# First keys loaded a step before first values, and two signs moved from the first network into the attention

## Chip, core and metric

One core of a Trainium2 chip runs the whole kernel. The metric is the device time in microseconds; of the kernel before, three runs are known, with a median of 729.78 us (726.8 to 729.82).

## What is computed

The reference is a gated block in two layers on x, 8 batches of 256 rows of 512:

```
x = x + tanh(g_xattn[0]) * L0_xattn(ctx, ctx, layernorm(x))   # long convolution of k*v, times q
x = x + tanh(g_ffn[0])   * L0_ffn(layernorm(x))                # 512 -> 1408 -> 512, ternary weights
x = x + tanh(g_xattn[1]) * L1_xattn(layernorm(x), ctx, mask)   # softmax over 256 context rows
x = x + tanh(g_ffn[1])   * L1_ffn(layernorm(x))                # 512 -> 2048 -> 512, one-bit weights
```

The last network uses `sign(w) * mean(|w|)` for each of its weights w1, w2 and w3. So signs of 3 x 2048 x 512 weights must be made at some time before it, and for w3 the sum of absolute values too. The attention of a batch needs the context twice: transposed as keys (cT) and as values (cN).

## The kernel before

The kernel keeps x in SBUF as 16 tiles of 128 rows (NT = 16) and goes through four stages: the convolution over 32 heads, the first network, the attention, the second network. The order of instructions is written out by hand: the program calls them in the order in which each engine is to run them, and every engine works through its own list in order. Engines wait for each other through semaphores only.

**The first network** is the loop over t from 0 to 16 (from L996). In step t TensorE makes the up products of tile t (`up_block`, L860, three blocks of columns 0, 512 and 1024), ScalarE applies SiLU (L868), VectorE multiplies (L869). In the same step the hidden rows of tile t - 1 are quantised: VectorE finds their maximum and the scale (L518 to L522), ScalarE rounds (L1019), POOL clips (L1037), SP starts a DMA transpose (`hqT`, L1039). One step later they are multiplied down (`down0`, L877), and one step after that added to x (`residual`, L228). In step 16 the attention's first work is mixed in: the table for Exp is loaded (L211), and the scores of tiles 0 and 1 (L951) are made between the last up product and the down product of tile 14. The down product of tile 15 follows in step 1 of the attention.

**The signs.** `w1_signs(k)` (L838) issues on SP the load of piece k, 256 KB, into one of three buffers (`p_st`, L844), and returns a function that lets ScalarE make the signs (L848) and, for the 16 pieces of w3, the sum of absolute values (L850). There are 48 pieces. Each step from 3 to 15 loads two, and the step after makes their signs; the last two, loaded in step 15, are made in the attention. The attention takes its number of loads per step from the list `SIGNS` and makes in step t what was loaded in step t - 1. In steps 1 to 15 one sign comes after eT, before the exponentials, and the others come at the end of the step.

**The attention** is a loop over t from 0 to 17 (from L1202). A full step has on TensorE: the transposes of the exponentials of tile t - 1 (L972), the scores of tile t (L951), the transposes of the normalised x of tile t + 2 (L940) and the readout of tile t - 1 (L980). ScalarE has eT (L974), a sign, the exponentials (L966), the normalised x of tile t + 3 (L201), and another sign. In the steps in `BY_POOL` the normalised x is made by POOL instead (L932). Keys and values of a batch serve two tiles and have two buffers each; those of batch t/2 + 1 are loaded in even and odd steps (L899, L904), the masks two batches ahead by POOL's own DMA (L909).

All loads, the transposes and the stores share SP's one queue and its order; masks go through POOL's queue. The lines that the change touches are L1044 (keys and values of batch 0, in step 14), L1083 (pool opened in step 13), L1088 (loads of pieces) and L1199 to L1200 (`SIGNS`, `BY_POOL`).

Of the kernel before, what the change touches and what calls it, by code (L numbers as in the profile page):

```python
# [23 lines left out]
NT = B * S // P  # L24
# [18 lines left out]
def flamingo_gated_kernel(  # L43
# [17 lines left out]
    def pool(stack, name, bufs, **kw):  # L61
        return stack.enter_context(tc.tile_pool(name=name, bufs=bufs, **kw))
# [146 lines left out]
    def load_table(func):  # L209

        nc.scalar.activation(junk1, ln_eps, func)  # L211
# [303 lines left out]
    def row_max(v, tag):  # L515

        am = small.tile([P, 1], F32, tag="am" + tag, name="am")
        nc.vector.tensor_reduce(am, v, AX.X, ALU.max, apply_absolute_value=True)  # L518
        inv = small.tile([P, 1], F32, tag="inv" + tag, name="inv")
        nc.vector.tensor_scalar(inv, am, Q_EPS, 1.0 / 127.0, ALU.max, ALU.mult)  # L520
        sc = small.tile([P, 1], F32, tag="sc" + tag, name="sc")
        nc.vector.reciprocal(sc, inv)  # L522
        return inv, sc

    def front_norm(k):
        xn0[k] = pf.tile([P, L], F32, tag="xn", name="xn2")
        if k < GRP:
            ln_apply_act(xn0[k], order0[k], *firsts[k // 2], k % 2)
        else:
            ln_apply_act(xn0[k], order0[k], *st0[k // GRP][1:], k % GRP)  # L530

    def front_max(k):
        am0[k] = row_max(xn0[k], "x")
# [320 lines left out]
    def up_block(xqT, f1, hh, f0):  # L854
        fw = min(512, FF0 - f0)
        pa = ps_mm.tile([P, 512], F32, tag="mm", name="pa")
        pb = ps_mm.tile([P, 512], F32, tag="mm", name="pb")
        for i, pp in ((0, pa), (1, pb)):
            for c in range(NL):
                nc.tensor.matmul(  # L860
                    pp[:, :fw],
                    xqT[:, c, :],
                    w0q[i][:, c, f0 : f0 + fw],
                    start=(c == 0),
                    stop=(c == NL - 1),
                )
        sl = p2.tile([P, 512], F32, tag="sl", name="sl")
        nc.scalar.activation(sl[:, :fw], pa[:, :fw], AF.Silu, scale=f1[:, 0:1])  # L868
        nc.vector.scalar_tensor_tensor(  # L869
            hh[:, f0 : f0 + fw], pb[:, :fw], f1[:, 1:2], sl[:, :fw],  # L870
            op0=ALU.mult, op1=ALU.mult,
        )
# [24 lines left out]
    def load_keys(b):  # L897
        cT = p3.tile([P, NL, S], F32, tag="cT", name="cT")
        nc.sync.dma_start(out=cT.rearrange("p c m -> p (c m)"), in_=ctx_t[b])  # L899
        return cT  # L900

    def load_values(b):
        cN = p3.tile([P, S // P, L], F32, tag="cN", name="cN")
        nc.sync.dma_start(out=cN, in_=ctx_n[b].rearrange("(c p) d -> p c d", p=P))  # L904
        return cN
# [13 lines left out]
    def batch_gate(neg):  # L919

        valid = small.tile([P, 1], F32, tag="valid", name="valid")
        nc.vector.tensor_reduce(valid, neg, AX.X, ALU.max)
        gv = small.tile([P, 1], F32, tag="gv", name="gv")
        nc.vector.tensor_scalar(gv, valid, 0.0, gate_x[1], ALU.is_equal, ALU.mult)
        return gv

    def normalised3(t, by_pool=False):
        xn = p3.tile([P, L], F32, tag="xn", name="xn3")
        rstd, nmr = st3[t // GRP][1:]
        if by_pool:  # L930
            c = slice(t % GRP, t % GRP + 1)
            nc.gpsimd.tensor_scalar(xn, xs[:, t, :], rstd[:, c], nmr[:, c], ALU.mult, ALU.add)  # L932
        else:
            ln_apply_act(xn, t, rstd, nmr, t % GRP)
        return xn
# [12 lines left out]
    def scores(xT, cT):  # L948
        ps = ps_mm.tile([P, 512], F32, tag="mm", name="ps")
        for c in range(NL):  # L950
            nc.tensor.matmul(  # L951
                ps[:, :S], xT[:, c, :], cT[:, c, :], start=(c == 0), stop=(c == NL - 1)
            )
        return ps
# [41 lines left out]
    for t in range(NT + 1):  # L996
        new = t + 2 < NT
        if t < NT:
            hh = p2.tile([P, FF0], F32, tag="hh", name="hh")
        if new and t > 0:  # L1000
            front_norm(t + 2)
        if t > 1:
            inv, sc = row_max(h_[t - 1], "h")
        if t == NT:
            xn_[2] = normalised3(2)
            load_table(AF.Exp)
            gates3 = {0: batch_gate(negs[0])}
            ps_ = {k: scores(xT_.pop(k), keys[0]) for k in range(2)}
        if t < NT:
            up_block(*x0[t], hh, 0)  # L1010
        if t == 0:
            front_norm(t + 2)
        if t == 1:

            ln_finish(*FINISH[0])
            inv, sc = row_max(h_[0], "h")
        if 1 <= t:
            q = p1.tile([P, FF0], I8, tag="i8h", name="i8h")
            nc.scalar.activation(q, h_.pop(t - 1), AF.Copy, scale=sc)  # L1019
        if t == NT - 2:  # L1020
            xn_ = {k: normalised3(k) for k in range(2)}
        if t >= 3:
            residual(order0[t - 3], *d_.pop(t - 3))
        back = BACK.get(t, [])
        if len(back) == 3:
            sums.append(odd_back(odds[back[0]]))
        if new:
            front_max(t + 2)
        if t < NT:
            up_block(*x0[t], hh, 512)  # L1030
        if t == NT - 1:
            xT_ = {k: x_transposed(xn_.pop(k), True) for k in range(2)}
        if new:
            front_int(t + 2)
        if 1 <= t:
            b = p2.tile([P, FF0], BF16, tag="qh", name="qh0")
            nc.gpsimd.tensor_scalar(b, q, 127.0, -128.0, ALU.min, ALU.max)  # L1037
            bT = p_hq.tile([P, NF0, P], BF16, tag="hqT", name="hqT")
            nc.sync.dma_start_transpose(out=bT, in_=b)  # L1039
            f3 = small.tile([P, 1], F32, tag="f3", name="f3")  # L1040
            nc.gpsimd.tensor_scalar(f3, inv, gw0, None, ALU.mult)
            hq_[t - 1] = (bT, f3)
        if t == NT - 2:
            keys, values = {0: load_keys(0)}, {0: load_values(0)}  # L1044
        if new:
            front_turn(t + 2)
        for add in sums:
            add()
        sums = []
        if back:  # L1050
            sums.append(odd_back(odds[back[-2]]))
        if t > 2:
            hqT, f3 = hq_.pop(t - 2)
            d_[t - 2] = (down0(hqT), f3)
        if t in FINISH and t > 0:
            ln_finish(*FINISH[t])

        for k in STATS3.get(t, ()):
            ln_moments_of(st3, natural, k, "3")
        if t > 0:  # L1060
            for k in STATS0.get(t, ()):
                ln_moments_of(st0, order0, k, "0")
        if t < NT:
            up_block(*x0.pop(t), hh, 1024)
            h_[t] = hh
        if t == 2:

            hqT, f3 = hq_.pop(0)
            d_[0] = (down0(hqT), f3)
        if back:  # L1070
            sums.append(odd_back(odds[back[-1]]))
        for add in sums:
            add()
        sums = []
        if t == 0:
            clip_by_act(2, 3)
        if t == 3:
            s_conv.close()
            wp1 = pool(ctx, "w1", 1, reuse_waits="tile")
            w1q = [wp1.tile([P, NL, FF1], F32R, name=f"w1_{i + 1}") for i in range(2)]  # L1080
            p_st = pool(s_att, "w1st", 3, reuse_waits="tile")
        if t == NT - 3:
            p3 = pool(s_att, "p3", 2, reuse_waits="tile")  # L1083
        if t < NT:
            for make in signs:
                make()
            signs = []
        if 3 <= t < NT:  # L1088
            signs = [w1_signs(made + k) for k in range(2)]
            made += 2  # L1090
        if t == NT - 2:
            bytes_ = {b: load_mask(b) for b in range(2)}
        if t == NT - 1:
            negs = {0: key_mask(bytes_.pop(0))}
        if t == NT:
            negs[1] = key_mask(bytes_.pop(1))
# [99 lines left out]

    SIGNS = [0, 2, 2, 2, 2, 1, 2, 1, 1, 2, 1, 1, 2, 2, 1]  # L1199
    BY_POOL = {5, 7, 10}  # L1200
    e_, r_ = {}, {}
    for t in range(NT + 2):  # L1202

# [32 lines left out]
        if t + 3 < NT:  # L1236
            xn_[t + 3] = normalised3(t + 3, t in BY_POOL)
        if t > 0:
# [37 lines left out]
        if t == NT:  # L1276
            mean_w1(2)
            nc.vector.tensor_scalar(gw1, wmean1[:, 2:3], gate_f[1], None, ALU.mult)
        if t < len(SIGNS):
            signs += [w1_signs(made + k) for k in range(SIGNS[t])]  # L1280
            made += SIGNS[t]
        if t == NT - 4:
# [217 lines left out]
```

## Time and profile before

| | |
|---|---|
| Median of three runs | 729.78 us |
| The profiled execution, as timed | 731.69 us |
| Its span in the trace | 729.8 us, granted TensorE clock 0.992 |
| ScalarE busy | 371.6 us (51%) |
| Up products of the first network, first to last | 181.1 to 299.5 us |
| Last down product of the first network (in the attention) | 312.3 to 314.9 us |
| Scores of the attention, first to last | 300.5 to 369.1 us |
| Signs (L848) | 48 of 0.62 us, from 220.5 to 371.7 us |
| DMA moved | 99.36 MB, mean 136 GB/s |

Times are measured from the start of the span. In a timeline, a row gives the start, the time, the engine, the source line, the operation, what it writes and reads, and in brackets how long the engine sat idle ahead of it and whose event ended that. In the rows of SP the time is that of issuing; when the bytes arrive is in the trace's DMA records. The chain of waits is followed back from the end of the program: each row is the work, or the wait for a transfer, that the next row could not start without.

### The profile page before, as it was taken

The numbers are of one execution on the slowest core, as the hardware profiler recorded it, in microseconds if no ns is written. First come the engines' busy times: TensorE is split into PE (matmuls) and PEld (weight loads), VectorE is DVE, ScalarE is ACT, GpSimd is POOL, SyncE is SP. The second block draws the span as 40 slices with busy tenths as digits, with TensorE's granted clock in tenths as the row PEclk, the third lists the DMA queues.
The fourth block names the chain that finished last, engine by engine and source line by source line (L and its number), as shares of the span: only waits on it lengthen the run. The fifth ranks groups of instructions, "written<-read, shape, count | busy, mean of one in ns | idle before, by whom it ended". The sixth has DMA issues, their size and how long they took to land.

```text
span 729.8 us, 10128 instructions
## 1 busy us (share of the span) xinstructions
PE 713.4 (98%) x3200; PEld 532.0 (73%) x3200; DVE 598.6 (82%) x1224; ACT 371.6 (51%) x669; POOL 260.8 (36%) x366
## 2 busy tenths in 40 slices
PE   7999999999899999899999999999999999999997
PEld 6777777777454444556668888888888888888885
DVE  5799888999788888777868988988888988777965
ACT  5577887879777777657652222322222332212322
POOL 4788997989874535245300020000200002000000
PEclk8999999999999999999999999999999999999999
DMA  5775676831136565797704455544553444554443
GB/s 196 238 240 159 188 266 202 281 85 32 35 84 139 141 142 141 159 279 219 225 27 96 103 110 110 115 96 110 113 115 83 110 103 104 118 110 91 102 90 86
DMA packets 149970, 99.36 MB, mean 136 GB/s; under 512 B 83806, under 2 KB 127838, under 8 KB 149918
## 3 DMA queue, kind: packets, MB, share of 16 engines
q1 hardware_dynamic: 149608, 98.38, 51.2%
q0 software_dynamic: 256, 0.26, 1.0%
q8 instruction: 25, 0.41, 0.2%
q14 instruction: 27, 0.22, 0.1%
q10 hardware_dynamic: 54, 0.08, 0.1%
HBM read 75.58 MB, written 5.03 MB: 110 GB/s over the span
## 4 chain that ended last, share of the span: by engine, by line
PE 82%; DVE 5%; DMA 4%; POOL 3%; issue 3%; ACT 2%; SPq 0%; DVEq 0%; ACTq 0%; POOLq 0%
PE y L349 17%; PE po L1375 16%; PE pb L1181 15%; PE pa L1181 15%; PE po L877 4%; PE pa L860 4%; PE pb L860 4%; PE po L980 2%; PE ps L951 2%; DMA w1st<-in_L_w3t 2%; DMA hqT<-qh 1%; POOL kv L326 1%; PE tr L416 1%; POOL prod L394 1%; DMA sT<-d 1%
## 5 line engine op out<-in xcount | busy, mean ns | idle before, releaser
L349 PE MATMUL y<-kv,toep 128*128 128x288 f32 x640 | 161.1, 409 | 0.9 <-DVE prod L384 0.7
L349 PEld LDWEIGHTS y<-kv,toep 128*128 128x128 f32 x640 | 120.1, 191 | 33.5 <-ACT qx L313 0.9
L1189 ACT ACTIVATE sl<-pa,wmean 128x512 f32<-128x512 f32 x64 | 44.0, 688 | 195.1 <-PE pa L1181 195.1
L1375 PE MATMUL po<-w,lo 128*128 128x512 f32 x256 | 99.9, 390 | 0.0
L1375 PE MATMUL po<-w,hi 128*128 128x512 f32 x256 | 99.6, 389 | 0.0
L181 POOL TENSOR_TENSOR nwt<-rstd 128x4 f32<-128x4 f32 x33 | 6.6, 199 | 235.1 <-DVE rstd L176 233.2
L326 POOL TENSOR_TENSOR kv<-cx 128x1024 f32<-128x1024 f32 x32 | 60.6, 1895 | 24.2 <-ACT cx L313 24.0
L1181 PE MATMUL pa<-w,hi 128*128 128x512 f32 x256 | 69.2, 392 | 0.0
L1181 PE MATMUL pb<-w,hi 128*128 128x512 f32 x256 | 68.6, 390 | 0.1
L1181 PE MATMUL pa<-w,lo 128*128 128x512 f32 x256 | 68.5, 389 | 0.0
L1181 PE MATMUL pb<-w,lo 128*128 128x512 f32 x256 | 68.4, 389 | 0.0
L860 PEld LDWEIGHTS <-xqT 128*128 128x128 bf16 x384 | 37.9, 99 | 41.2 <-issue 3.1
L394 POOL TENSOR_TENSOR prod<-prod 128x1024 f32<-128x1024 f32 x28 | 66.3, 2368 | 0.0
L1155 ACT CAST hi<-v 128x512 fp32r<-128x512 f32 x64 | 39.2, 622 | 47.9 <-DVE v L1365 47.9
L1193 DVE SCALAR_TENSOR_TENSOR hh<-pb,wmean,sl 128x512 f32<-128x512 f32 x64 | 47.8, 747 | 14.7 <-PE pb L1181 14.5
L1375 PEld LDWEIGHTS po<-w,lo 128*128 128x128 f32 x256 | 48.0, 188 | 10.9 <-DVE lo L1160 1.0
L1181 PEld LDWEIGHTS pa<-w,hi 128*128 128x128 f32 x256 | 47.8, 188 | 10.8 <-ACT hi L1155 0.6
L1181 PEld LDWEIGHTS pb<-w,hi 128*128 128x128 f32 x256 | 48.0, 188 | 10.5 <-DVE hh L1193 0.6
L1181 PEld LDWEIGHTS pa<-w,lo 128*128 128x128 f32 x256 | 48.1, 188 | 10.0
L1375 PEld LDWEIGHTS po<-w,hi 128*128 128x128 f32 x256 | 48.1, 188 | 9.9
L1181 PEld LDWEIGHTS pb<-w,lo 128*128 128x128 f32 x256 | 48.0, 188 | 10.0
L371 DVE TENSOR_TENSOR prod<-y,qx 128x512 f32<-128x512 f32 x64 | 43.8, 684 | 8.6 <-ACT y L359 4.4
(163 smaller groups left out, 1345.3 us busy)
## 6 DMA issues: line engine op xcount, KB each, us to landing
sT<-d SPq DMA_DIRECT2D x64, 256.0 KB
toep<-ssm_skip SPq DMA_DIRECT2D x31, 256.0 KB
ch<-in_ctx_heads SPq DMA_DIRECT2D x32, 128.0 KB
w1a<-in_L_w1t SPq DMA_DIRECT2D x8, 512.0 KB
w1a<-in_L_w2t SPq DMA_DIRECT2D x8, 512.0 KB
w1st<-in_L_w1t SPq DMA_DIRECT2D x16, 256.0 KB
w1st<-in_L_w2t SPq DMA_DIRECT2D x16, 256.0 KB
cT<-in_ctx_t SPq DMA_DIRECT2D x8, 512.0 KB
```

Of the source, the lines that this page charges most:

```text
L326: nc.gpsimd.tensor_tensor(kv[:, :, 0 : ND * HD].rearrange("p a (i d) -> p a i d", d=ND), cx[:, :, 0:HD].unsqueeze(3).to_broadcast([P, NL * ...
L349: nc.tensor.matmul(y[:, k, :, W0 : W0 + NPAIR], toeps[h][:, d * P : (d + 1) * P], kvs[h][:, mi * B : (mi + 1) * B, :].rearrange("p b n -> ...
L371: nc.vector.tensor_tensor(prod[:, 0, r, :, :], yv[:, :, W0 : W0 + ND * HD].rearrange("p a (i d) -> p a i d", d=ND), view(q, [HX, n], [1, H ...
L394: nc.gpsimd.tensor_tensor(flat[0], flat[0], flat[1], ALU.add)
L860: nc.tensor.matmul(pp[:, :fw], xqT[:, c, :], w0q[i][:, c, f0 : f0 + fw], start=(c == 0), stop=(c == NL - 1),)
L877: nc.tensor.matmul(po, hqT[:, c, :], w0q[2][:, c, :], start=(c == 0), stop=(c == NF0 - 1))
L951: nc.tensor.matmul(ps[:, :S], xT[:, c, :], cT[:, c, :], start=(c == 0), stop=(c == NL - 1))
L1155: nc.scalar.copy(hi, v)
L1181: nc.tensor.matmul(pp, xT[k][:, c, :], w1q[i][:, c, f0 : f0 + 512], start=(c == 0 and k == 0), stop=(c == NL - 1 and k == 1),)
L1189: nc.scalar.activation(sl, pa, AF.Silu, scale=wmean1[:, 0:1])
L1193: nc.vector.scalar_tensor_tensor(hh, pb, wmean1[:, 1:2], sl, op0=ALU.mult, op1=ALU.mult)
L1375: nc.tensor.matmul(po, hT[b][k][:, c, :], w1q[2][:, b * NL + c, :], start=(b == 0 and c == 0 and k == 0), stop=(b == NB - 1 and c == NL - ...
```

## The change

Four edits. The keys of batch 0 are loaded at the end of step 13, before that step's two pieces, instead of in step 14 just before the values. Step 14 loads no pieces, so step 15 makes no signs, and every later piece is loaded and made by a later entry of the lists. `SIGNS` has one load more in step 0 and one more in step 5. POOL makes the normalised x of attention step 6 instead of that of step 5.

```diff
         if t == NT - 2:
-            keys, values = {0: load_keys(0)}, {0: load_values(0)}
+            values = {0: load_values(0)}
...
         if t == NT - 3:
             p3 = pool(s_att, "p3", 2, reuse_waits="tile")
+            keys = {0: load_keys(0)}
         if t < NT:
             for make in signs:
                 make()
             signs = []
-        if 3 <= t < NT:
+        if 3 <= t < NT and t != NT - 2:
             signs = [w1_signs(made + k) for k in range(2)]
             made += 2
...
-    SIGNS = [0, 2, 2, 2, 2, 1, 2, 1, 1, 2, 1, 1, 2, 2, 1]
-    BY_POOL = {5, 7, 10}
+    SIGNS = [1, 2, 2, 2, 2, 2, 2, 1, 1, 2, 1, 1, 2, 2, 1]
+    BY_POOL = {6, 7, 10}
```

The pieces that each step loads, before and after:

| | step 13 | 14 | 15 | attention 0 | 1 to 4 | 5 | from 6 |
|---|---|---|---|---|---|---|---|
| before | 20, 21 | 22, 23 | 24, 25 | none | 26 to 33 | 34 | 35 on |
| after | 20, 21 | none | 22, 23 | 24 | 25 to 32 | 33, 34 | 35 on |

Pieces 16 to 31 are of w2, those from 32 on of w3. The number of instructions on each engine stays the same.

## The prediction

> **What bounds the kernel now.** I read the page first, then the chain of waits in order of time, then the timelines of single engines in the stretch that the diff touches.
>
> ```profile
> span 729.8 us, 10128 instructions
> PE 713.4 (98%) x3200; PEld 532.0 (73%) x3200; DVE 598.6 (82%) x1224; ACT 371.6 (51%) x669; POOL 260.8 (36%) x366
> ```
>
> TensorE fills 98% of the span, so a change without a matmul in it can only win where TensorE waits. The order of TensorE's and of VectorE's instructions is the same in both kernels; only the orders on ScalarE (ACT), SyncE (SP) and GpSimd (POOL) differ. The chain of waits leaves TensorE twice between 299 and 313 us, where the first network's last steps (t = 15 and 16) meet the attention:
>
> ```profile
> 299.02 5.36 DMA hqT<-qh
> ...
> 304.43 2.55 PE po L877 x11
> ...
> 308.75 3.50 DMA hqT<-qh
> ...
> 312.30 2.56 PE po L877 x11
> ```
>
> Two transposes of the quantised hidden rows each hold back a down product (L877). The second row, on an empty queue, takes 3.50 us; the first takes 5.36. The SP timeline says what lay ahead of it, and when each was issued:
>
> ```profile
> 290.52 1.39 SPq L1039 DMA_TRANSPOSE hqT<-qh  x1
> 291.95 0.84 SPq L899 DMA_DIRECT2D cT<-in_ctx_t  x1
> 292.85 0.43 SPq L904 DMA_DIRECT2D cN<-in_ctx_n  x1
> 293.37 1.72 SPq L844 DMA_DIRECT2D w1st<-in_L_w2t  x2
> 299.02 2.10 SPq L1039 DMA_TRANSPOSE hqT<-qh  x1
> 301.21 2.15 SPq L844 DMA_DIRECT2D w1st<-in_L_w2t  x2
> ```
>
> Keys, values and two sign pieces (512+512+256+256 KB, section 6 of the page) are issued within 3.2 us, behind a transpose. The trace's DMA records show their bytes moving from about 295 to 302.5 us; the keys' last part lands at 300.37, the pieces at 302.36 and 303.05, and the transpose only after them at 304.38. The timelines of TensorE, ScalarE and VectorE show who waits:
>
> ```profile
> 300.50 3.69 PE L951 MATMUL ps<-cT,xT 128*128 128x256 f32 x16 [0.65 <-DMA cT<-in_ctx_t]
> 312.30 2.55 PE L877 MATMUL po<-w,hqT 128*128 128x512 bf16 x11 [1.14 <-DMA hqT<-qh]
> ```
> ```profile
> 302.38 1.32 ACT L848 ACTIVATE w<-w1st 128x512 fp32r<-128x512 f32 x2 [2.56 <-DMA w1st<-in_L_w2t]
> 303.61 0.80 ACT L201 ACTIVATE xn<-xs,nmr,rstd 128x512 f32<-128x512 f32 x1
> 304.43 1.28 ACT L211 ACT_TABLE_LOAD   x1
> 305.72 0.20 ACT L211 ACTIVATE junk<-ln_eps 128x1 f32<-128x1 f32 x1
> 305.83 1.45 ACT L1019 ACTIVATE i8h<-hh,sc 128x1408 int8<-128x1408 f32 x1
> ```
> ```profile
> 302.45 0.17 DVE L522 RECIPROCAL sc<-inv 128x1 f32<-128x1 f32 x1
> ```
>
> The cause of the second stall is in the middle fence. ScalarE works in order: two signs wait 2.56 us for their pieces, and behind them queue a normalisation, the table load and the last quantisation (L1019). The scale it needs was ready at 302.62, but it starts at 305.83, 3.2 us late, and through POOL (L1037) it makes the last transpose as late.
>
> **The change part by part.** The sum is made against the profiled execution, span 729.8 us, 731.69 us as timed; the median of the three runs shown is 729.78 (726.8 to 729.82), so a span saving is taken off 729.78.
>
> *The two signs of step 14.* Their loads (293.37) and their ScalarE work (302.38, with the wait) leave this place. After the last activation of step 15 (L868, 299.24 to 299.72) ScalarE goes on with xn 0.7, table 1.28 and junk 0.2, so it is free by 302.0, and the quantisation starts when its scale is there: 302.62 + 0.10 (the step before: scale done 295.98, start 296.08) = 302.72. POOL starts 1.56 later (296.08 to 297.64 before), the transpose is issued 1.38 after that (297.64 to 299.02): 305.66. It lands 3.50 later at 309.16 and its product starts at 309.2 instead of 312.30: **3.1 us** earlier. Here a rule speaks against the sum. The Trainium skill, page "ScalarE: Activation LUTs", section "What ACT_TABLE_LOAD costs", charges a switch of table at 1283 ns plus a drain of 1380 ns. By it ScalarE would be free at 303.3, past the scale, and the saving would be 2.5 us, an estimate. The trace has the load at 304.43, 0.02 after the 0.80 row in front of it, and the next row 1.29 later: no drain shows, so I take 1.28.
>
> *Does TensorE get there in time?* Scores (L951) can start when the last up block ends (299.04 + 0.65) and ScalarE's xT (second copy done by 299.1) is there: 299.72 instead of 300.50, provided the keys are present. Sixteen matmuls at 3.44 back to back (300.50 to 303.94) end at 303.16. The first delayed transpose, issued at 299.02 on a queue that holds only values by then, takes the 3.50 of the empty-queue row and lands at 302.5, so the down product runs 303.16 to 305.54, 1.27 earlier than now. Then transposes of xn (0.44), of the exponentials (0.22; their maximum is ready on VectorE at 304.84, the exponentials at 305.4), the next transposes when VectorE has emptied the bank (306.87), and the readout 307.44 to 309.16. So TensorE is free at 309.2 too. The two bounds meet; 3.1 us stands, and what is late next is either.
>
> *The keys a step ahead.* Issued at about 286.4, ahead of step 13's two pieces. There the cost is bounded by the hole in the queue:
>
> ```profile
> 290.00:292.00 2.00, 2.00 (x13) 1.12 (x12) 0.93 (x2) 1.80 (x4) 1.89 (x4) 1.00 0.15 30
> ```
>
> The last columns are DMA share and GB/s. Before, step 13's pieces landed at 289.87 and 290.49 (landing records). 512 KB more at the 400 GB/s that this trace's full half-microseconds show is 1.3 us, so they land at 291.2 and 291.8. ScalarE takes them at 291.71 and some 0.5 later; behind them on ScalarE stand the first activation of step 15 (292.75) and then 2.64 us of idling before L1019, which covers it. The transpose issued at 290.52 shows its first packets at 291.69 anyway; it landed by 295.01, its product starts at 296.01. Bounds: nothing, and, if the 1 MB needs twice the 4.1 us that 0.5 MB took from issue to landing, a product up to 1.7 us late. I take nothing, since the hole is there in the row. A gain beyond the 0.78 counted is excluded, because scores need xT. SP's other passed entry is the mask load on POOL, which is not moved.
>
> *The signs in the attention.* Sixteen steps of 4.1 us on TensorE (0.22 + 1.73 + 0.44 + 1.72 in the chain). Two pieces more: one loaded in step 0, one in step 5, so step 1 makes three signs and step 6 two. A sign is 0.62, with its absolute sum 1.45 (L848, L850). Step 6 loses a normalisation (0.80) to POOL (0.77), step 5 gets it back and swaps one w3 piece for a w2 piece. Step 5 on ScalarE then is 0.62 + 1.45 + 0.80 + 0.70 + 0.36 = 3.9 and step 6 is 2.9 + 0.70 + 0.36 = 4.0, both under 4.1. In step 1 the third sign waits for its piece, issued behind the next keys: it lands about 311.5, the sign ends near 312.4, and eT behind it is due for the readout at 313.9. Cover 1.1 us, so nothing on the path; if the piece came 2 us later, 0.9. On SP, step 1's loads wait until signs free their buffers (to about 311), and behind them stand the keys of the third batch, first read in step 4, some 10 us on. POOL's mask load of step 6 now stands behind the moved normalisation, 0.8 us later. That bears on these waits:
>
> ```profile
> 342.35 0.63 ACT L848 ACTIVATE w<-w1st 128x512 fp32r<-128x512 f32 x1 [1.62 <-DMA w1st<-in_L_w3t]
> 359.58 0.63 ACT L848 ACTIVATE w<-w1st 128x512 fp32r<-128x512 f32 x1 [2.14 <-DMA w1st<-in_L_w3t]
> ```
>
> TensorE lost 0.28 at the first (344.28 against 344.00) and 0.76 at the second (361.51 against 360.75). The packets of mask and piece overlap between 338 and 341. A later mask lets the first piece pass: a gain of 0.28, else at worst 0.5 more loss. I take the gain, since the piece's own queue is short there. The second is left as it is. Sum: 3.1 + 0.3 = 3.4 us, 729.78 - 3.4 = **726.4 us**.
>
> A second rule bears on the queue. "DMA: Bandwidth & Descriptors", in "Rules for kernel authors", says that a transpose next to ordinary DMAs needs nothing. That concerns order, not time: read as free company, the first transpose would gain nothing from an emptier queue. The rows say 5.36 behind the bulk, 3.50 without. By the rule read so, the down product stays at 304.43, the readout ends 1.2 later, and the total gain is about 2.2; by the rows 3.4. I take the rows.
>
> **Rivals.**
> *More than that:* with masks and loads falling otherwise, both attention waits vanish, and with them the 0.38 us before 319.33: 3.1 + 0.28 + 0.76 + 0.38 = 4.5, so 725.3. For it: these waits are accidents of one engine's late packets. Against: their buffers turn over as before.
> *Given back to bandwidth:* 512 KB move from a network step into the attention, where 310 to 330 us already runs at some 270 GB/s. If that is the limit, 1.9 us come back and 1.5 remain: 728.3. Against: SP there mostly waits for ScalarE to free a buffer, not for bytes.
> *Slower:* all three sign buffers are full when the attention starts, so every load waits for the sign before it, and every sign of steps 1 to 7 for its load; ScalarE, in order, holds up eT and the exponentials. At the 0.76 of the 359.58 row, seven steps cost 5.3, net +1.9: 731.7; at the whole 2.14, +11.6. It decides from 0.49 us a step. For it: such waits exist in the trace. Against: in steps 2 to 5 of before, with the same two pieces a step, just one such wait (317.33) shows, with no TensorE idling behind it.
> *It does not do what it says:* step 13's traffic delays the 290.52 transpose by 1.7 and the rest moves with it: net 1.7, 728.1.
>
> **How the numbers follow.** 0.5% is 3.65 us, about what a measurement of this kernel can tell from no change, so 726.13 and 733.43 are the borders. Main case 726.4 with its own range 725.4 to 727.4, chance 0.47, a little under half beyond the border. More: 0.30, all beyond. Bandwidth or step 13: 0.10. Slower: 0.13, somewhat over half within 0.5%. Faster 0.22 + 0.30 = 0.52; slower 0.06; the rest, 0.42, same. The range takes in 'more' with the 3 us by which the runs shown differ, half of it below: 723.8; above it reaches past bandwidth into the slower case's lower half: 730.0.
>
> **What would show it.** Right: no w1st wait on ScalarE near 302, L1019 started near 302.7, scores near 299.7, the last two down products near 303.2 and 309.2. Step 13 is wrong if the product at 296.01 waits. The attention is wrong if L848 rows in its first eight steps show DMA waits with TensorE idling at tre (L972) behind them.

## The result and the profile after

| | before | after |
|---|---|---|
| Median | 729.82 us (13 runs, 726.8 to 732.12) | 726.0 us (13 runs, 724.78 to 728.54) |
| Profiled execution, as timed | 731.69 us | 727.47 us |
| Its span | 729.8 us | 725.6 us |

The ratio is 0.9959, with a 95% interval of 0.9944 to 0.9973: a saving of 3.0 us (2.0 to 4.1) where 3.4 was forecast; the two medians lie 3.8 us apart, inside that interval. It can be measured, and the best estimate is less than 0.5%.

From the page of the kernel after, the head and the busy time of the engines (the two instructions more than before are no engine's work: the counts behind each x are the same):

```profile
span 725.6 us, 10130 instructions
...
PE 710.6 (98%) x3200; PEld 530.8 (73%) x3200; DVE 598.7 (83%) x1224; ACT 371.5 (51%) x669; POOL 260.1 (36%) x366
```

The chain of waits in order of time (start, length, what):

```profile
301.76 2.37 PE po L877 x11
...
305.91 1.72 PE po L980 x4
307.67 2.56 PE po L877 x11
...
331.84 6.96 DMA w1st<-in_L_w3t
338.83 0.64 ACT w L848
339.49 0.72 ACT w1st L850 x2
340.21 0.50 ACT s L966 x2
340.76 0.44 PE tre L972 x2
```

Both `hqT` transfers are gone from it: through the last two down products of the first network the chain stays on TensorE, but for one copy by ScalarE (0.38 us, L974). But one new transfer has come in, at 331.84: a piece of w3, whose late arrival holds ScalarE and then TensorE at 340.76.

The timeline of ScalarE around the table load, then that of SP (time of issue), then that of TensorE:

```profile
298.17 0.80 ACT L201 ACTIVATE xn<-xs,nmr,rstd 128x512 f32<-128x512 f32 x1
298.99 1.28 ACT L211 ACT_TABLE_LOAD   x1
300.29 0.20 ACT L211 ACTIVATE junk<-ln_eps 128x1 f32<-128x1 f32 x1
301.16 1.47 ACT L1019 ACTIVATE i8h<-hh,sc 128x1408 int8<-128x1408 f32 x1 [0.67 <-DVE sc L522]
```
```profile
297.48 1.37 SPq L1039 DMA_TRANSPOSE hqT<-qh  x1
298.90 1.27 SPq L844 DMA_DIRECT2D w1st<-in_L_w2t  x2
304.10 1.39 SPq L1039 DMA_TRANSPOSE hqT<-qh  x1
```
```profile
298.14 3.62 PE L951 MATMUL ps<-cT,xT 128*128 128x256 f32 x16
301.60 2.54 PE L877 MATMUL po<-w,hqT 128*128 128x512 bf16 x11
...
307.67 2.55 PE L877 MATMUL po<-w,hqT 128*128 128x512 bf16 x11
...
314.70 0.44 PE L972 MATMUL tre<-ident,s 128*128 128x128 f32 x2 [0.38 <-ACT s L966]
...
340.76 0.44 PE L972 MATMUL tre<-ident,s 128*128 128x128 f32 x2 [1.22 <-ACT s L966]
```

The quantisation L1019 no longer stands behind two signs. ScalarE is free early and waits 0.67 us for VectorE's scale. The scores and both down products have no idle time in brackets ahead of them.

**How the profiles are compared.** This profile reaches the down product of tile 12 at 286.47, that of before at 288.01, long ahead of anything the change touches. So I count from that product on. The table shows how much earlier (minus) TensorE started its work than in the first profile of before. "Before again" and "after again" are second profiles of the same two kernels; "tre k" are the transposes of the exponentials of tile k (L972), made in attention step k + 1.

| | before again | after | after again | keys only | signs only | signs late | few masks | masks on SP |
|---|---|---|---|---|---|---|---|---|
| scores (L951) | +0.26 | -0.82 | -0.82 | -0.82 | -0.82 | +0.02 | -0.82 | -0.82 |
| down product, tile 14 | +0.30 | -1.29 | -1.29 | -1.29 | -1.29 | +0.07 | -1.29 | -1.29 |
| down product, tile 15 | +0.32 | -3.09 | -3.08 | -1.68 | -3.10 | -1.92 | -3.10 | -3.08 |
| tre 2 | +0.32 | -3.09 | -3.04 | -1.68 | -3.10 | -1.94 | -3.10 | -2.73 |
| tre 8 | +0.05 | -1.98 | -1.61 | -1.83 | -2.15 | -2.21 | -3.38 | -3.02 |
| second network, first up product | -0.76 | -2.80 | -2.42 | -2.65 | -2.97 | -3.09 | -4.25 | -3.89 |

Two things are to be read in it. By tile 15 the change brings 3.09 us in both profiles, counted from the first profile of before; counted from before again, whose own stretch is 0.3 us longer, it is 3.4. By tre 8 it has lost 1.1 (2.0 left) and 1.5 (1.6 left) of that again.

### The profile page after: what moved, and what is told of

It reads as the page before. It is cut to its first block, busy times and chain, and to the rows that moved or that the text cites. A ratio compares the mean times of both kernels' runs of the same rounds, so it can differ in the third digit from the quotient of the medians.

```text
span 725.6 us, 10130 instructions
## 1 busy us (share of the span) xinstructions
PE 710.6 (98%) x3200; PEld 530.8 (73%) x3200; DVE 598.7 (83%) x1224; ACT 371.5 (51%) x669; POOL 260.1 (36%) x366
## 4 chain that ended last, share of the span: by engine, by line
PE 92%; DVE 2%; DMA 2%; ACT 2%; issue 1%; POOL 0%; SPq 0%; DVEq 0%; ACTq 0%; POOLq 0%
PE y L349 22%; PE po L1376 16%; PE pb L1182 15%; PE pa L1182 15%; PE po L877 5%; PE pa L860 5%; PE pb L860 5%; PE ps L951 3%; PE po L980 3%; DMA w1st<-in_L_w3t 1%; PE tr L416 1%; PE tr_back L424 1%; PE tr L940 1%; DMA sT<-d 1%; DMA ch<-in_ctx_heads 1%
```

## Experiments: the two bounds at the first network's end

The theory: two signs in ScalarE's order cost the last down product 3.1 us, the loads ahead of the first transpose cost the first one 1.3. The rivals put the gain on the keys alone, or see the move of the loads as needless.

**Keys only.** Before, with this edit alone:

```diff
         if t == NT - 2:
-            keys, values = {0: load_keys(0)}, {0: load_values(0)}
+            values = {0: load_values(0)}
...
         if t == NT - 3:
             p3 = pool(s_att, "p3", 2, reuse_waits="tile")
+            keys = {0: load_keys(0)}
```

> The kernel before with one edit: the keys of batch 0 loaded in step 13, signs and lists as before. Theory (the gain is the emptied queue and the freed ScalarE, and the two signs of step 14 cause both): moving 512 KB away brings step 14's two pieces and the first transpose some 1.3 us forward, so ScalarE's wait near 302 shrinks from 2.56 to about 1.3, scores start 0.7 earlier, the first of the two last down products 1.2 earlier, the second 1.3 earlier. Total 1.3 us, ratio 0.998. Rival (the keys are the gain, since the scores wait for them): the whole 3.1 us, ratio 0.996.

Measured: 729.51 us (20 runs) against 730.0, ratio 0.9988 (0.9971 to 1.0005), so the times alone don't show a gain. In the profile the two down products come 1.29 and 1.68 earlier, where 1.2 and 1.3 were expected. The timeline of ScalarE, then that of TensorE:

```profile
298.86 1.32 ACT L848 ACTIVATE w<-w1st 128x512 fp32r<-128x512 f32 x2 [0.89 <-DMA w1st<-in_L_w2t]
...
300.91 1.28 ACT L211 ACT_TABLE_LOAD   x1
...
302.31 1.45 ACT L1019 ACTIVATE i8h<-hh,sc 128x1408 int8<-128x1408 f32 x1
```
```profile
308.78 2.55 PE L877 MATMUL po<-w,hqT 128*128 128x512 bf16 x11 [1.13 <-DMA hqT<-qh]
```

The signs now wait 0.89 us instead of 2.56, because their pieces no longer queue behind the keys. But they still stand ahead of L1019, and the last transpose still stops TensorE for 1.13. So 1.41 of the 3.09 us stay lost as long as the signs stand there.

**Signs only.** Before, with the other edits and the keys left in step 14:

```diff
-        if 3 <= t < NT:
+        if 3 <= t < NT and t != NT - 2:
...
-    SIGNS = [0, 2, 2, 2, 2, 1, 2, 1, 1, 2, 1, 1, 2, 2, 1]
-    BY_POOL = {5, 7, 10}
+    SIGNS = [1, 2, 2, 2, 2, 2, 2, 1, 1, 2, 1, 1, 2, 2, 1]
+    BY_POOL = {6, 7, 10}
```

> The kernel before with the signs of step 14 moved (and the two lists as in the changed kernel), keys still beside the values in step 14. Theory: with 512 KB less in the queue the keys land before 299.7 anyway (they are first in it), the transpose on an empty queue takes 3.5 us, the last quantisation starts when its scale is ready: the second down product 3.1 us earlier, as in the changed kernel, ratio about 0.996. Rival (the keys matter by themselves): scores still wait 0.65 us and the gain is 2.4 or less.

Measured: 729.03 us (20 runs), ratio 0.9976 (0.9961 to 0.9992). All rows of the table down to the second down product are those of after, to 0.01 us. So in the profile moving the signs gives the whole 3.1, and moving the keys then adds nothing: without the two pieces the keys are there by 300.03, and the scores start at 300.30 with no idle time. The times leave this less certain: a ratio of about 0.996 was expected, and 0.9976 is nearer to no change than the 0.9959 of after, though the two intervals overlap.

**Signs late.** Before, with only ScalarE's order changed: the two signs of step 14's pieces, which stood in step 15, go behind L1019. Every load stays where it was.

```diff
             nc.scalar.activation(q, h_.pop(t - 1), AF.Copy, scale=sc)
+            if t == NT:
+                signs.pop(0)()
+                signs.pop(0)()
...
-        if t < NT:
+        if t < NT - 1:
             for make in signs:
                 make()
             signs = []
         if 3 <= t < NT:
-            signs = [w1_signs(made + k) for k in range(2)]
+            signs += [w1_signs(made + k) for k in range(2)]
```

> The kernel before with all loads where they were; only the making of step 14's two pieces on ScalarE moves from before the table load to just behind the last quantisation (L1019). Theory: the quantisation starts at 302.7, so ScalarE's share of the gain appears without the queue's: the first transpose still takes 5.4 us and holds the first product at 304.4, the second product is bounded by TensorE at about 310.4, 1.9 us earlier. Rival (the queue is the whole cause, ScalarE's order only follows): no gain, 0.0 us.

Measured: 728.7 us (20 runs), ratio 0.9972 (0.9955 to 0.9989). The first down product does not move (+0.07), the second comes 1.92 earlier. The timeline of ScalarE:

```profile
303.26 1.47 ACT L1019 ACTIVATE i8h<-hh,sc 128x1408 int8<-128x1408 f32 x1 [0.68 <-DVE sc L522]
```

L1019 starts as soon as the scale is there, as in after, but TensorE comes to the last product only at 310.9, since the first transpose still lands late behind the bulk. This separates the two bounds: a new order on ScalarE with the old loads gives 1.92, the keys out of the way with the old order (which shortens the signs' wait too) 1.68, both bounds together 3.09. It is no sum; the later of the two counts each time.

## Experiments: the loss at attention step 9

TensorE's list between tre 7 and tre 8 is 4.10 us long. What it took beyond that: before 0.28 and 0.02 in its two profiles, keys only 0.13, signs late 0.00, all with the old lists; after 1.39 and 1.72, signs only 1.23, all with the new lists. ScalarE's row ahead of it in after (its timeline), then one from the attention's start, for comparison:

```profile
338.83 0.63 ACT L848 ACTIVATE w<-w1st 128x512 fp32r<-128x512 f32 x1 [2.73 <-DMA w1st<-in_L_w3t]
```
```profile
310.91 0.63 ACT L848 ACTIVATE w<-w1st 128x512 fp32r<-128x512 f32 x1 [1.24 <-DMA w1st<-in_L_w2t]
```

The wait at 310.91 is that of the third sign in step 1. TensorE has nothing in brackets behind it. The wait at 338.83 is too long to hide: behind it in ScalarE's order stand the exponentials (L966) whose transposes TensorE needs. This piece is loaded in step 7, and its signs are made in step 8, so it is called the piece of step 7 below.

**Few masks.** After, with the mask loads of batches 2 to 7 left out; those batches use the masks of batches 0 and 1.

```diff
             if b < B:
                 keys[b] = load_keys(b)
-            if b + 1 < B:
-                bytes_[b + 1] = load_mask(b + 1)
...
-                negs[b + 1] = key_mask(bytes_.pop(b + 1))
+                negs[b + 1] = key_mask(bytes_[(b + 1) % 2])
```

> The changed kernel with the mask loads of batches 2 to 7 left out: every later batch takes the mask of batch 0 or 1 again, so six of eight masks are not the reference's. In the changed kernel ScalarE waits 2.73 us at 338.83 for the first piece of attention step 7 and TensorE idles 1.22 us behind it. Theory (the mask packets of POOL's queue slow that piece): the wait falls under 1 us, TensorE idles under 0.3 us, the total falls by about 1 us against the changed kernel. Rival (the piece is late because its buffers turn over late, or by chance of one DMA engine): wait and idling stay.

Measured: 726.15 us (19 runs), ratio 0.9946 (0.9929 to 0.9963): 3.9 us below before (2.7 to 5.2), where after is 3.0 below (2.0 to 4.1). The loss is 0.00, and no wait for w3 is left in the attention. The windows view shows what happens while a mask comes in. Last two columns: DMA share and GB/s. First this kernel, then after, whose TensorE is at the same place to 0.03 us:

```profile
334.00:335.00 1.00, 1.00 (x4) 0.46 (x3) 1.00 (x2) 1.00 (x3) 0.00 (x0) 1.00 1.05 404
335.00:336.00 1.00, 1.00 (x6) 0.72 (x5) 0.86 (x6) 0.97 (x5) 0.00 (x0) 1.00 0.96 309
```
```profile
334.00:335.00 1.00, 1.00 (x4) 0.50 (x3) 1.00 (x2) 1.00 (x3) 0.00 (x0) 1.00 1.20 152
335.00:336.00 1.00, 1.00 (x7) 0.68 (x5) 0.86 (x6) 0.97 (x4) 0.00 (x0) 1.00 0.78 80
```

In after, 16 packets of a mask, 2 KB each, are in flight from 334.07 to 337.33 by the trace's DMA records, 1.25 us each on average against 0.10 for packets of the same size on SP's queue. The DMA share stays high, yet 232 KB pass in two microseconds instead of 713. The missing 481 KB are 1.2 us at 400 GB/s, an estimate. The rate by itself proves nothing against the masks: from 332 to 333 it is as low in this kernel (92 GB/s), with no mask packet in flight. What counts is when the piece lands, which is taken up at the end of this section.

**Masks on SP.** After, with one word changed; nothing is left out.

```diff
-        nc.gpsimd.dma_start(out=mu, in_=mask[b].partition_broadcast(P))
+        nc.sync.dma_start(out=mu, in_=mask[b].partition_broadcast(P))
```

> The changed kernel with one line changed: the masks are loaded from SP's queue instead of POOL's. Theory (it is the mask transfers of POOL's queue that slow the keys, values and pieces around them): as in the run with few masks, ScalarE's wait for the piece of attention step 7 falls under 1 us, TensorE idles under 0.3 us there, first and second last down products as in the changed kernel; ratio about 0.9945, about 1 us better than the changed kernel. Rival (a mask costs the 16 DMA engines the same from any queue, or now holds up SP's own order): no better than the changed kernel, ratio 0.996 or above.

Measured: 726.53 us (7 runs) against 730.91 on that chip, ratio 0.9941 (0.992 to 0.9962), the lowest ratio of the study. The loss at step 9 is 0.00. A smaller one comes in step 3 (0.57 us idle, 0.38 in after), where the masks now stand in the queue of the pieces; that they cause it was not tested. The timeline of TensorE:

```profile
318.07 0.44 PE L972 MATMUL tre<-ident,s 128*128 128x128 f32 x2 [0.57 <-ACT s L966]
```

The mask bytes are still loaded here and the loss is away, so it goes with the masks on POOL's queue, not with their bytes as such. That rests on one profile of each of the two kernels. The intervals of both overlap that of after, so the times alone don't show that either is faster than after.

**Both kernels again, one profiled execution each.** No edit.

> The kernel before, unchanged, for a second profile. If the waits of ScalarE for w3 pieces at attention steps 8 and 12 (1.62 and 2.14 us) belong to the program, they come back within 0.3 us; if they are chance of single transfers, they change by a microsecond. The stretch from 296 to 313 us should come back within 0.2 us in all its steps.

> The changed kernel, unchanged, for a second profile: the last two down products 1.3 and 3.1 us earlier than before, counted from the down product of step 14, within 0.1 us; the wait of 2.73 us for the piece of attention step 7 comes back if it belongs to the change, and moves by about a microsecond if it is chance.

Before again took 728.63 us, after again 730.1, so single executions can stand the other way round. In before again the stretch from 296 to 313 us comes 0.26 to 0.32 us later, more than the 0.2 expected. The wait at step 8 comes back (1.36 for 1.62), the one at step 12 does not. In after again the two down products are where they were, and the loss is there, and larger (TensorE's timeline):

```profile
343.36 0.44 PE L972 MATMUL tre<-ident,s 128*128 128x128 f32 x2 [1.55 <-ACT s L966]
```

In before again TensorE loses nothing at step 13, where the prediction had read a loss of 0.76 behind the wait at 359.58. That loss was chance of one profile.

**Which part of the new lists?** After, with step 5's normalisation given back to POOL in place of step 6's: `BY_POOL = {5, 7, 10}`.

> The changed kernel with BY_POOL = {5, 7, 10} as before. ScalarE's step 6 then has two w3 pieces and a normalisation: 2.9 + 0.8 + 0.7 + 0.36 = 4.8 us against TensorE's 4.1, so it should fall 0.7 us behind in step 6 and TensorE idle by up to that near attention step 7; POOL's mask load of step 6 goes 0.8 us sooner. Theory of the moved mask: the wait for the piece of step 7 falls to about 1.6 us as in the kernel before. Rival (the wait does not depend on the mask's 0.8 us): it stays near 2.7 us.

One execution: 726.32 us, and no loss at step 9. That spoke for `BY_POOL` as the cause, so I ran the same kernel again, several times.

> The changed kernel with BY_POOL = {5, 7, 10} once more, timed and with a second profile. In the first profile TensorE did not idle at attention step 9 where the changed kernel idles 1.22 and 1.55 us. If that belongs to BY_POOL, it does not idle again, and the ratio is near that of the run with masks on SP, 0.994 to 0.995; if it was chance, about 1 us of idling comes back and the ratio is 0.996.

Measured: 728.42 us (12 runs) against 731.34, ratio 0.9955 (0.9936 to 0.9974), that of after. The loss is back at 1.39. ScalarE's timeline in the first profile, then in the second, then TensorE's in the second:

```profile
337.30 0.63 ACT L848 ACTIVATE w<-w1st 128x512 fp32r<-128x512 f32 x1 [1.10 <-DMA w1st<-in_L_w3t]
```
```profile
340.56 0.63 ACT L848 ACTIVATE w<-w1st 128x512 fp32r<-128x512 f32 x1 [2.08 <-DMA w1st<-in_L_w3t]
```
```profile
342.49 0.44 PE L972 MATMUL tre<-ident,s 128*128 128x128 f32 x2 [1.16 <-ACT s L966]
```

One kernel, once a wait of 1.10 that hides and once one of 2.08 that does not: my first reading falls. The loss comes without the new `BY_POOL` too, so that edit is not its cause.

**Less work for ScalarE in steps 5 and 6.** After, with `BY_POOL = {5, 6, 7, 10}`: if buffers came free too late because ScalarE is full in step 5, this should help.

> The changed kernel with BY_POOL = {5, 6, 7, 10}: POOL makes both normalisations, so ScalarE's step 5 is light again, and POOL's mask load of step 6 stays behind a normalisation. Theory A (late mask): about 1.2 us of idling stay in step 9. Theory B (buffers freed late by ScalarE's step 5): the idling goes.

Measured: 728.83 us (10 runs), ratio 0.9956 (0.9933 to 0.9979); loss 1.03. It doesn't help enough for that theory.

**The mask ahead of the normalisation.** After, with POOL issuing the mask in even steps before its normalised x, not behind it:

```diff
             e_[t] = exponentials(*s_nmx)
+        if t % 2 == 0 and t // 2 + 2 < B:
+            bytes_[t // 2 + 2] = load_mask(t // 2 + 2)
         if t + 3 < NT:
             xn_[t + 3] = normalised3(t + 3, t in BY_POOL)
...
-            if b + 1 < B:
-                bytes_[b + 1] = load_mask(b + 1)
```

> The changed kernel, BY_POOL = {6, 7, 10}, with POOL's mask load of an even step issued ahead of the normalisation of that step instead of behind it; so the mask of step 6 goes 0.8 us sooner and ScalarE's list stays as changed. Theory A (the mask stands late and runs into the piece of step 7): the wait at that piece falls to about 1.1 us and TensorE does not idle in step 9. Theory B (ScalarE's step 5, which got the normalisation back, frees its piece buffers later, so the loads behind them on SP go later): wait of 2.5 us and 1.2 us of idling stay.

Measured: 728.4 us (10 runs), ratio 0.9964 (0.9941 to 0.9987). Loss 0.28 at step 9, behind a wait of 1.66, and 0.35 one step earlier: less than in after, and not gone. Inconclusive.

**The fifth step's extra piece put elsewhere.** After, with that piece loaded in step 10:

```diff
-    SIGNS = [1, 2, 2, 2, 2, 2, 2, 1, 1, 2, 1, 1, 2, 2, 1]
-    BY_POOL = {6, 7, 10}
+    SIGNS = [1, 2, 2, 2, 2, 1, 2, 1, 1, 2, 2, 1, 2, 2, 1]
+    BY_POOL = {7, 10, 11}
```

> The changed kernel with the second extra piece loaded in attention step 10 instead of step 5, and POOL's normalisation for the step that makes it: SIGNS = [1, 2, 2, 2, 2, 1, 2, 1, 1, 2, 2, 1, 2, 2, 1], BY_POOL = {7, 10, 11}. BY_POOL and the mask's place alone did not explain the idling of TensorE before the exponentials' transposes of step 9 (0.28 and 0.0 us before; 1.2 to 1.7 us in the changed kernel's two profiles and in the run with the signs' edit alone; 0.0 where POOL loads few masks or none). Theory C (the extra piece of step 5 crowds the queue ahead of the piece of step 7 while a mask transfers): idling of 0.3 us or less there, down products as in the changed kernel; it may come up again near step 12; ratio 0.995. Rival (the one-piece lag from step 0 on does it, or chance): idling of about 1 us in step 9 stays.

Measured: 728.93 us (12 runs) against 730.7, ratio 0.9971 (0.9955 to 0.9988). ScalarE's last three waits for w3 in its timeline up to 366 us:

```profile
333.71 0.63 ACT L848 ACTIVATE w<-w1st 128x512 fp32r<-128x512 f32 x1 [0.37 <-DMA w1st<-in_L_w3t]
...
350.18 0.63 ACT L848 ACTIVATE w<-w1st 128x512 fp32r<-128x512 f32 x1 [0.33 <-DMA w1st<-in_L_w3t]
...
358.11 0.63 ACT L848 ACTIVATE w<-w1st 128x512 fp32r<-128x512 f32 x1 [0.16 <-DMA w1st<-in_L_w3t]
```

Its profile has no loss at step 9, which fits the extra piece as the cause. The timed ratio is no better than that of after (the intervals overlap), and as shown above one profile without a loss proves little. So the extra piece fits as the cause and is not shown to be it.

**When the piece lands.** All fourteen profiles can be asked when the piece of step 7 was issued on SP and when the last of its 16 parts landed (landing records). Times are in us, counted from the start of tre 7:

| | issued | issue to landing | landed | loss at step 9 |
|---|---|---|---|---|
| before | -3.43 | 5.87 | 2.43 | 0.28 |
| before again | -3.43 | 5.60 | 2.17 | 0.02 |
| keys only | -3.43 | 5.71 | 2.28 | 0.13 |
| signs late | -3.43 | 3.71 | 0.28 | 0.00 |
| after | -3.43 | 6.96 | 3.54 | 1.39 |
| after again | -2.86 | 6.73 | 3.87 | 1.72 |
| signs only | -3.11 | 6.49 | 3.38 | 1.23 |
| `BY_POOL` with 5 for 6, first | -2.80 | 4.74 | 1.94 | 0.00 |
| the same, second | -2.40 | 5.93 | 3.53 | 1.39 |
| `BY_POOL` with 5 and 6 | -2.85 | 6.03 | 3.19 | 1.03 |
| mask ahead | -3.41 | 5.84 | 2.43 | 0.28 |
| piece put in step 10 | -3.47 | 4.15 | 0.68 | 0.00 |
| few masks | -3.43 | 3.99 | 0.57 | 0.00 |
| masks on SP | -3.44 | 4.20 | 0.77 | 0.00 |

Wherever the piece lands later than 2.15 us after tre 7, the loss is the excess, to 0.01 us. So a piece issued 3.43 us ahead may take 5.58 us. Two things use that up. The first is the time to landing: with a mask of POOL's queue in flight it is 3.71 to 6.96 us (twelve profiles), without one 3.99 and 4.20. Three of the four profiles with the old lists have 5.60 to 5.87, so before already stood at the limit. The second is the issue. The load needs a buffer that ScalarE frees; ScalarE's timeline and that of SP, in before and then in after again:

```profile
333.62 0.19 ACT L850 ACTIVATION_READ_ACCUMULATOR w1st<-w1st 128x1 f32 x1
```
```profile
336.47 0.47 SPq L844 DMA_DIRECT2D w1st<-in_L_w3t  x1
```
```profile
334.47 0.19 ACT L850 ACTIVATION_READ_ACCUMULATOR w1st<-w1st 128x1 f32 x1
```
```profile
334.68 0.33 SPq L844 DMA_DIRECT2D w1st<-in_L_w3t  x1
```

In before the buffer is free 2.7 us ahead of the load, in after again 0.02. In all four profiles with the old lists it is 2.5 to 2.7, in all nine with the new ones 0.02 to 0.35, and 1.85 with the extra piece in step 10. So the new lists take the slack away, and any delay of ScalarE in step 6 goes on to this load: in five of the nine profiles it is issued 0.3 to 1.0 us later than in before.

## Why the prediction was right, and where not

**The main step held, in its working as well.** On the clock of before (1.54 us later than that of after), with the forecast in brackets: L1019 at 302.70 (302.72), scores at 299.68 (299.72), first down product 303.14 (303.16), last transpose issued at 305.64 (305.66), last down product 309.21 (309.2). The transposes landed 3.49 and 3.52 us after their issue (3.50), by the trace's landing records; so with less ahead of it in the queue the first transpose is shorter, 3.49 for 5.36. That the two bounds meet was right too: the last transpose lands at 307.62, the readout ahead of the product ends at 307.63. "Signs late" and "keys only" show each bound alone.

**The table load.** The row was right: junk starts 1.30 after the load of 1.28, and L1019 then waits only for its scale. By the rule of the Trainium skill ("ScalarE: Activation LUTs", "What ACT_TABLE_LOAD costs"), with a drain of 1380 ns, ScalarE would have been free at about 301.9, an estimate, not by the 301.16 at which L1019 starts.

**Step 13.** Nothing was lost: the product after it starts 8.00 us after the one before it, in both kernels. Its two pieces landed at 291.16 and 292.30 on the clock of before (291.2 and 291.8 forecast). In the first profile of after this was close: the transpose ahead of that product took 5.37 us instead of 4.50 and landed 0.13 us before it was needed, not 1.00. In after again it took 4.36, with 1.14 us to spare.

**The slower rival** did not decide. In steps 1 to 5 ScalarE waits 1.24, 1.17, 0.29, 0.60 and 0.30 us for pieces, but TensorE is not idle longer behind them than before (0.38 at 314.70, as before). The third sign in step 1 ended at 313.08 on the clock of before, 0.7 later than forecast, and still under its cover of 1.1.

**The step that failed** is "I take the gain, since the piece's own queue is short there": 0.28 us to be gained at step 9 from a mask that comes later. Its sign was wrong. What ScalarE has to wait for there grew from 1.62 to 2.73 and 2.56 us, and TensorE lost 1.1 and 1.4 more than in the first profile of before. The mask was later, as I said: POOL issued it 3.66 and 2.59 us ahead of tre 7, where it was 4.04 and 3.80 before. The mechanism I named (mask packets over a piece) fits: without masks on POOL's queue the piece took 3.99 and 4.20 us, with them and the new `SIGNS` 4.74 to 6.96; but not every mask slows it (3.71 in "signs late"). That a later mask lets the piece pass is what did not happen. My bound of "at worst 0.5 more loss" was too narrow. I also wrote of these waits that "their buffers turn over as before", and they don't: the piece's buffer is freed 0.02 to 0.35 us before its load with the new lists, 2.5 to 2.7 with the old.

**The sum.** 3.1 less some 1.1 to 1.4 is 1.7 to 2.0, under the 3.0 (2.0 to 4.1) of the timed runs. Pairs of single profiles give 1.66 to 2.80 from tile 12's product to the second network. The two overlap between 2.0 and 2.8, and no run here narrows that further. The loss varies from one execution to the next (0.00 and 1.39 in one and the same kernel), and I have no mean of it over the timed runs. The forecast of 3.4 came near the measured 3.0 although it counted a small gain where there was a loss. That is partly luck: put right by the profiles' loss, its own sum would have been 1.7 to 2.0.

**What stays open:** why the piece takes longer from issue to landing with the new lists. A loss over 1.0 stands in five of seven profiles with the new `SIGNS` and masks on POOL's queue, at most 0.28 in four with the old. A later issue explains 0.3 to 1.0 us in four of those five; in the first profile of after the issue is not late, and the whole loss lies in the 6.96 us to landing. It isn't `BY_POOL`; the piece added in step 5 fits, from one profile. Which of the piece's packets wait behind which of the mask's was not settled.

## What to carry to other kernels

Where an engine works in order, ask what its next instruction waits for and what stands behind that: here two signs that nobody needed for a long time held the last quantisation. Making them later gained 1.92 us, and moving their loads away as well 3.1. A product that is late for two reasons is freed by as much as the later of them allows, so work out both before adding. A transfer that hides in one profile is not hidden for good: look at a wait with little cover in more than one execution before a gain or a loss is put on it.

## What the runs showed of the hardware

A small broadcast from POOL's queue can slow a load on SP's queue a good deal. The 256 KB of one piece took 3.99 and 4.20 us from issue to landing with no mask on POOL's queue, and 3.71 to 6.96 us in twelve profiles with one. With sixteen packets of a mask in flight, the core's DMA moved 152 and 80 GB/s in two successive microseconds, where it moved 404 and 309 without them.

The granted clock gives single profiles a spread of its own. In the first steps of the network TensorE sits idle for 3 us, in before and in after alike (its timelines):

```profile
194.73 1.16 PE L860 MATMUL pa<-w,xqT 128*128 128x512 bf16 x4 [3.05 <-ACT sl L868]
```
```profile
194.79 1.02 PE L860 MATMUL pa<-w,xqT 128*128 128x512 bf16 x4 [3.04 <-ACT sl L868]
```

Soon after, from 195.5, TensorE ran at half clock for 3.4 us in before; in after, no such stretch lies there. The windows view, before and then after (the column ahead of the last two is the granted clock):

```profile
194.00:198.00 4.00, 3.27 (x11) 1.68 (x11) 2.35 (x3) 4.00 (x8) 3.49 (x8) 0.69 0.17 35
```
```profile
194.00:198.00 4.00, 3.21 (x17) 1.74 (x17) 2.28 (x3) 4.00 (x8) 3.48 (x8) 1.00 0.16 33
```

In these 4 us TensorE gets through 11 matmuls in the one and 17 in the other. The stretch stands in twelve of the fourteen profiles, after again among them, so it isn't the change that took it away. From the network's first up product to the down product of tile 12 those twelve take 106.86 to 106.92 us; the two without it (after, and the second one of `BY_POOL` with 5 for 6) take 105.25 and 105.29. So the stretch costs 1.6 us. It accounts for the 1.54 us by which the two first profiles differ before step 13: at the first up product they are still within 0.08 us (181.14 and 181.22). Why it stays away now and then is open.
